# A four-layer graph network on one core: in the fourth layer, the products that sum ReLUs to scores go from the middle to the end of the first ten steps

## The chip, the core and the metric

The kernel runs on one core of a Trainium2 chip. The core has a matrix engine (TensorE, PE in the profile), a vector engine (VectorE, DVE), an engine for functions of one element (ScalarE, ACT), GpSimd (POOL) and queues that start transfers (SyncE, SP). Each engine works through its own list of instructions in order, and waits where an operand or a buffer is not ready. TensorE writes into PSUM, which has few banks; VectorE and ScalarE read the results from there ("evict" them) and so free the bank for the next product.

The metric is the device time of one execution in microseconds, as the median of several runs. Lower is better.

## The reference

Four layers are added to `x` (128 graphs of 64 nodes with 256 features) one after another. Each takes a layer norm and a ReLU of `x` first. The change is in the last one, graph attention over 512 edges with four heads:

```python
def _L3_gnn_ref(H, W_lin, W_val, a, W_out, A0, src, dst):
    Xq = (H @ W_lin.T).reshape(bt, n, h, dh)
    Xv = (H @ W_val.T).reshape(bt, n, h, dh)
    Qs = Xq[:, src]
    Kt = Xq[:, dst]
    e = jnp.einsum('behd,hd->beh', jax.nn.leaky_relu(Qs + Kt, LRELU_SLOPE), a)
    e = e + jnp.log(A0[src, dst] + EPS)[None, :, None]
    ...
    attn = ex / denom[src]
    Vt = Xv[:, dst].transpose(1, 0, 2, 3)
    Y = jax.ops.segment_sum(attn[..., None] * Vt, src, num_segments=n)
    Y = Y.transpose(1, 0, 2, 3).reshape(bt, n, d)
    return Y @ W_out.T
...
h = jnp.maximum(_layernorm(x, axis=-1), 0.0)
x = x + _L3_gnn_ref(h, L3_gnn_W_lin, L3_gnn_W_val, L3_gnn_a, L3_gnn_W_out, adj, L3_gnn_src, L3_gnn_dst)
```

`ex / denom[src]` is a softmax over the edges that leave one node. A leaky ReLU with slope 0.2 is 0.2 times its argument plus 0.8 times its ReLU, and the kernel uses it in that form.

## The kernel before

`x` lies in sixteen tiles X of 512 rows (128 partitions, four row blocks of 256). The fourth layer, `layer3` (L2439), runs 32 steps `g` of 256 rows, four graphs. Its parts, in the names that the trace shows:

- `score` (L2585): eight products of queries Q with an edge matrix (`ed_S2`, which adds the rows of source and target of each edge), each into a PSUM bank `ps` of its own, and eight ReLUs on ScalarE from `ps` to tiles `r`. There are seven `ps` banks and eight `r` tiles.
- `reduce` (L2606): eight products that multiply each `r` with the weights `a` (`ed_apad`) and add the result into the PSUM bank `acc`. Each has a stationary operand of 32 columns, so four stand side by side in the array. Eight steps share one `acc`; the first of the eight opens it. There is one such bank.
- `summed` (L2687), after every eighth step: one more product adds the linear part (`lin`) to `acc` and closes it. `softmax` (L2674) then reads `acc` with two scans, a maximum and a subtraction on VectorE (`sm_m`, `sm_e`, in `shifted`, L2691), takes Exp on ScalarE, and goes on with scans and reciprocals on VectorE.
- `edgewise` (L2703): two steps later `sm_e` is transposed and copied to `at`. `between` (L2715), `weighted` (L2743) and `output` (L2759) use it: VectorE spreads `at` over edges into tiles `aw`, TensorE gathers them (`aw` with `ed_ODT`), weights the values, and multiplies with the output matrix `w_o`. They lag ten steps behind (`LAG`, L2455; `v = g - LAG`), so in the first ten steps none of them runs.
- `back` (L2281): the layer before leaves its result in another layout (`big`). In each of steps 0 to 7 the next block is copied to `ls_t` (half on VectorE, half on ScalarE), transposed on TensorE (`ident` with `ls_t`) and added to X on VectorE. This is called the way back.
- `turned` (L2505), in even steps: the normed rows `h` are transposed (`ident` with `h`) to `hT`, one half evicted by VectorE and the other by ScalarE, and VectorE makes the sums `hS`.
- `queries` (L2535), in odd steps: queries and values of the next block from `hT` and `hS`, seven pairs of products by one level of Strassen-like sums, whose evictions go partly into each other (`XV`, `Q`). Its second half, `rest`, follows after `output` and `edgewise`, and ends with `linear` (L2569), which makes `lin`.
- `normed` (L2600), in odd steps: the layer norm of a later block (`n_st`, `n_mv`, `n_v`, `n_y` by Sqrt on ScalarE, `n_r`, `n_m`, then `h`).

In a step of the first ten the calls are `score`, `normed`, `reduce`, `summed` (step 7), `back` (steps 0 to 7), `turned` or `queries`, `edgewise` (step 9), `rest`, `softmax` (step 7).

The order on each engine comes from a scheduler that the tile framework runs over the whole program. It may take later instructions of another engine's list forward where operands allow; on TensorE the order of `layer3` is largely that of the calls. Buffers rotate in the order in which the program asks for them: an allocation of a `ps` bank waits for the readers of the one seven allocations earlier. The products of `reduce` take none of these seven.

Every operation is recorded through one helper, so nearly all lines of the profile say L799; one goes by the names of the tiles.

Of the kernel before, what the change touches and what calls it, by code (L numbers as in the profile page):

```python
# [842 lines left out]
class Plan:  # L843
# [56 lines left out]
    def rest(self):  # L900

        while any(self.queue.values()):
            for e in self.queue:
                self.fill(e, 1e9)
# [545 lines left out]
NG = 4  # L1450
# [15 lines left out]
class Kernel:  # L1466
# [972 lines left out]
    def layer3(self):  # L2439
        nc, o, io = self.nc, self.o, self.io  # L2440
        cx, (w,) = self.stage([("l3x", 1)], "tile")
        with cx:
            cy, pools = self.stage([("l3", 2), ("l3v", 2), ("l3s", 1), ("l3r", 6), ("l3ps", 7), ("l3cps", 1)], "tile")
            with cy:
                self.a02 = self.everywhere(w, "ed_a", io["L3_gnn_a"].rearrange("h d -> (h d)"))
                o.ts(self.a02[:], self.a02[:], 0.2, ALU.mult)
                self.drop, self.dropr = (w.tile([P, E], F32, name="ed_" + n) for n in ("drop", "dropr"))
                WQV = w.tile([P, 2, 2 * D], F32, name="w3_qv")
                for x, n in enumerate(("W_lin", "W_val")):
                    nc.sync.dma_start(WQV[:, :, x * D:(x + 1) * D],  # L2450
                                      io[f"L3_gnn_{n}_t"].rearrange("(k p) m -> p k m", p=P))
                WO = self.weights(w, "w3_o", io["L3_gnn_W_out_t"])


                st, LAG = {}, 10  # L2455
                self.turned(st, 0, *pools)
                WQV = self.sums3(w, WQV)
                self.queries(st, 0, WQV, *pools)()
                for g in range(8 * NG):
                    v = g - LAG  # L2460
                    ahead = (g + 1) // 2 if g % 2 and g + 1 < 8 * NG else None
                    self.score(st, g, *pools)
                    if g % 2 and g + 3 < 8 * NG:
                        self.normed(st, (g + 3) // 2, pools[0])
                    if v >= 1:
                        self.weighted(st, v - 1, *pools)
                    self.reduce(st, g, *pools)
                    if g == 4:
                        self.drops()
                    if v >= 0:  # L2470
                        self.between(st, v, *pools)
                    if g % 8 == 7 and g + 1 < 8 * NG:
                        self.summed(st, g // 8, *pools)
                    if g < 8:
                        self.back(8 + g, pools[4], "ps")
                    if ahead:
                        rest = self.queries(st, ahead, WQV, *pools)
                    elif g + 2 < 8 * NG:
                        self.turned(st, g // 2 + 1, *pools)
                    if g + 6 == 8 * NG:  # L2480

                        p = pools[4].tile([P, BT], F32, name="ps")
                        for c in range(4):
                            self.nc.tensor.transpose(p[:N, c * P:(c + 1) * P], self.OST[:, c, :], self.ident[:])
                        self.act_copy(self.cont[:N, :], p[:N, :])
                    if v >= 1 and g + 1 < 8 * NG:
                        self.output(st, v - 1, WO, *pools)
                    if g % 8 == 1 and 1 < g:
                        self.edgewise(st, g // 8 - 1, *pools)
                    if ahead:  # L2490
                        rest()
                    if g % 8 == 7 and g + 1 < 8 * NG:
                        self.softmax(st, g // 8, *pools)
                self.turn(st, WO, pools)
# [342 lines left out]
```

## Time and profile before

| | us |
|---|---|
| runs of the kernel before, median of 3 | 2264.54 |
| lowest and highest of them | 2262.23, 2266.95 |
| profiled execution | 2267.39 |
| its span | 2265.6 |
| fourth layer from the scores of step 0 to the end of the span | 1754.07 to 2265.6 |
| scores of step 10 begin | 1863.60 |

The profile lists, for each engine, how long it was busy, which groups of instructions cost most, who waited for whom, and the chain of work that ended last. A line of the timeline gives start, length, engine, source line, operation, output and inputs, tile shape and count, and in brackets the idle time before it with what ended it. Several products in a row are one line; their lengths overlap a little, so the distance from one line's start to the next one's is what a group takes. One product in float32 shows as two records.

The windows of the first ten steps, two steps to a row (columns: window, its length, busy time and instructions of PE, PEld, DVE, ACT and POOL, granted clock, share of the transfer engines, GB/s):

```profile
1754.07:1775.63 21.56, 21.56 (x117) 12.25 (x116) 13.17 (x33) 15.43 (x27) 0.00 (x0) 1.00 0.00 1
1775.63:1797.20 21.57, 21.57 (x117) 12.25 (x116) 14.55 (x36) 13.88 (x26) 0.00 (x0) 1.00 0.00 1
1797.20:1818.77 21.57, 21.57 (x117) 12.25 (x116) 14.13 (x34) 13.88 (x26) 0.00 (x0) 1.00 0.00 1
1818.77:1842.12 23.35, 23.01 (x119) 12.46 (x118) 16.29 (x36) 14.76 (x27) 0.00 (x0) 1.00 0.00 1
1842.12:1863.60 21.48, 20.18 (x105) 10.71 (x104) 18.46 (x42) 13.54 (x26) 0.00 (x0) 1.00 0.00 0
```

TensorE is busy throughout in the first three rows; the clock is full, and transfers play no part. The last two rows hold the first softmax.

### The profile page before, as it was taken

What the parts mean: (1) busy time and instruction counts of PE and PEld (TensorE: products, weight loads), DVE (VectorE), ACT (ScalarE), POOL (GpSimd) and SP (SyncE); (2) the same over time, 40 slices, a digit from 0 to 9 for tenths busy, and PEclk for the clock granted to TensorE, in tenths of its full rate; (3) what the DMA queues carried; (4) which work ended last, traced back from release to release, by engine and by line L of the source; (5) the groups of instructions that cost most, each with busy time, mean ns of one, the idle gap of its engine ahead of it and who ended that gap; (6) DMA issues with size and microseconds to landing.
All of it is one profiled execution on the core that took longest, in us unless ns stands there. A gap on an engine that the chain in (4) does not pass through costs nothing.

```text
span 2265.6 us, 33653 instructions
## 1 busy us (share of the span) xinstructions
PE 2222.2 (98%) x12617; PEld 1619.5 (71%) x12617; DVE 1611.1 (71%) x4068; ACT 1143.9 (50%) x2499; POOL 7.3 (0%) x33
## 2 busy tenths in 40 slices
PE   7999998999999999999999999999999999999999
PEld 4554444667777778888999999888887555555554
DVE  8877576888438786676766766666965688778667
ACT  5667864764436663444444444334533664444431
POOL 1000000000000000000000000000000000000000
PEclk9999999999999999999999999999999999999999
DMA  6000210121000000000100002000002000000001
GB/s 180 1 1 13 73 56 23 66 94 38 1 28 1 1 19 1 1 1 1 38 1 1 1 1 75 1 1 5 13 1 75 1 1 15 15 20 20 15 25 48
DMA packets 61070, 54.88 MB, mean 24 GB/s; under 512 B 15203, under 2 KB 58724, under 8 KB 60900
## 3 DMA queue, kind: packets, MB, share of 16 engines
q1 hardware_dynamic: 60900, 52.66, 7.5%
q8 instruction: 101, 1.65, 0.3%
q14 instruction: 69, 0.57, 0.1%
HBM read 35.86 MB, written 16.78 MB: 23 GB/s over the span
## 4 chain that ended last, share of the span: by engine, by line
PE 78%; DVE 4%; ACT 1%; issue 1%; ACTq 0%; DVEq 0%
PE ps L799 71%; PE pt L799 4%; PE acc L799 3%; DVE sm_m L799 1%; PE pe L799 1%; DVE aw L799 1%; DVE X L799 1%; DVE XV L799 0%; ACT ls_g L799 0%; ACT h L799 0%; DVE ls_g L799 0%; DVE lin_p L799 0%; DVE lin_s L799 0%; DVE hT L799 0%; DVE sm_e L799 0%
## 5 line engine op out<-in xcount | busy, mean ns | idle before, releaser
L799 ACT ACTIVATE ls_g<-ls_g,ls_b 128x512 f32<-128x512 f32 (+4 forms) x472 | 243.2, 565 | 154.7 <-DVE ls_g L799 152.9
L799 ACT ACTIVATE ls_g<-ps,ls_b 128x256 f32<-128x256 f32 (+3 forms) x268 | 115.3, 470 | 335.6 <-PE ps L799 332.5
L799 PE MATMUL ps<-z,w 128*128 128x512 f32 x512 | 257.2, 624 | 0.0
L799 PE MATMUL ps<-big,X 128*128 128x176 f32 (+3 forms) x848 | 212.7, 366 | 0.1
L799 DVE TENSOR_TENSOR ls_g<-ls_z,ps 128x512 f32<-128x512 f32 (+5 forms) x256 | 146.9, 579 | 91.6 <-PE ps L799 90.0
L799 PE MATMUL ps<-ls_tx,X 128*128 128x160 f32 (+2 forms) x960 | 206.8, 326 | 1.5 <-DVE ls_tx L799 0.9
L799 PE MATMUL ps<-X,X 128*128 128x160 f32 (+1 forms) x896 | 199.0, 306 | 0.0
L799 PE MATMUL ps<-X,ls_w 128*128 128x256 f32 x640 | 190.4, 379 | 0.0
L799 PEld LDWEIGHTS ps<-ls_tx,X 128*128 128x128 f32 x960 | 161.7, 190 | 16.4 <-DVE X L799 4.8
L799 DVE TENSOR_TENSOR aw<-at,ed_OST 128x1024 f32<-128x1024 f32 x128 | 150.3, 1219 | 28.7 <-PE ps L799 28.5
L799 PEld LDWEIGHTS ps<-big,X 128*128 128x128 f32 x848 | 146.0, 190 | 29.7 <-issue 19.4
L799 ACT ACTIVATE r<-ps 128x512 f32<-128x512 f32 x256 | 129.3, 625 | 63.0 <-PE ps L799 63.0
L799 DVE TENSOR_TENSOR X<-ls_g 128x1024 f32<-128x1024 f32 (+2 forms) x108 | 117.4, 1087 | 49.8 <-ACT ls_g L799 49.8
L799 PEld LDWEIGHTS ps<-X,X 128*128 128x128 f32 x896 | 148.5, 190 | 0.0
L799 PE MATMUL ps<-X,ls_s 128*128 128x256 f32 x480 | 142.3, 379 | 0.0
L799 PEld LDWEIGHTS ps<-z,w 128*128 128x128 f32 x512 | 87.6, 191 | 67.8 <-issue 60.6
L799 PE MATMUL ps<-ls_tx,ls_s 128*128 128x256 f32 x464 | 134.7, 379 | 0.0
L799 PEld LDWEIGHTS ps<-X,ls_w 128*128 128x128 f32 x640 | 121.4, 190 | 16.8 <-DVE X L799 0.3
L799 PE MATMUL ps<-ls_tx,ls_w 128*128 128x256 f32 x464 | 133.3, 380 | 0.1
L799 PE MATMUL ps<-big,ls_w 128*128 128x256 f32 x464 | 131.9, 379 | 0.8 <-ACT ls_z L799 0.8
L799 PE MATMUL ps<-ed_S,Q 64*128 64x512 f32 x512 | 121.4, 604 | 2.2 <-DVE hT L799 1.3
L799 PE MATMUL ps<-aw,ed_ODT 128*32 128x512 f32 x1024 | 121.7, 593 | 0.1
(552 smaller groups left out, 3946.4 us busy)
## 6 DMA issues: line engine op xcount, KB each, us to landing
X<-in_x_dram SPq DMA_DIRECT2D x32, 512.0 KB
xs<-X SPq DMA_DIRECT2D x16, 512.0 KB
X<-xs SPq DMA_DIRECT2D x16, 512.0 KB
out_dram<-X SPq DMA_DIRECT2D x31, 256.0 KB
X<-in_L_gnn_Wih_t_dram SPq DMA_DIRECT2D x4, 512.0 KB
ls_w<-in_L_gnn_Wih_t_dram SPq DMA_DIRECT2D x4, 512.0 KB
ls_w<-in_L_gnn_Whh_t_dram SPq DMA_DIRECT2D x4, 512.0 KB
w<-in_L_gnn_W_t_dram SPq DMA_DIRECT2D x2, 512.0 KB
```

The source lines that it names most:

```text
L799: i = method(*a, **kw)
```

## The change

In the steps in which nothing lags behind (`v < 0`, that is `g` from 0 to 9), `reduce` is called after `rest`, as the last work of the step on TensorE; in step 7 `summed` follows it there. From step 10 on the order is the old one. Nothing is computed differently.

```diff
                     if v >= 1:
                         self.weighted(st, v - 1, *pools)
-                    self.reduce(st, g, *pools)
+                    if v >= 0:
+                        self.reduce(st, g, *pools)
                     if g == 4:
                         self.drops()
                     if v >= 0:
                         self.between(st, v, *pools)
-                    if g % 8 == 7 and g + 1 < 8 * NG:
+                    if v >= 0 and g % 8 == 7 and g + 1 < 8 * NG:
                         self.summed(st, g // 8, *pools)
                     if g < 8:
                         self.back(8 + g, pools[4], "ps")
...
                         self.edgewise(st, g // 8 - 1, *pools)
                     if ahead:
                         rest()
+                    if v < 0:
+                        self.reduce(st, g, *pools)
+                        if g == 7:
+                            self.summed(st, 0, *pools)
                     if g % 8 == 7 and g + 1 < 8 * NG:
                         self.softmax(st, g // 8, *pools)
```

The scheduler's list moves other engines' work too. In the changed kernel's issue order ScalarE takes the first softmax's table load and Exp after the third ReLU of step 8 (before: ahead of all eight), and the first query eviction comes ahead of the normed rows `h`. VectorE runs the first softmax nearly without other work between its pieces, and copies `hT` ahead of the four reciprocals (before: behind them).

## The prediction

> **What bounds the kernel now.** I read the page first: TensorE is busy almost all the time, and the chain that ended last runs on it.
>
> ```profile
> PE 2222.2 (98%) x12617; PEld 1619.5 (71%) x12617; DVE 1611.1 (71%) x4068; ACT 1143.9 (50%) x2499; POOL 7.3 (0%) x33
> PE 78%; DVE 4%; ACT 1%; issue 1%; ACTq 0%; DVEq 0%
> ```
>
> A busy TensorE can still be one that crawls, so next I read the timeline of TensorE and ScalarE in the first ten steps of the fourth layer (1754.07 to 1863.60 us). Steps 0 and 1, then step 9 and a block of later steps:
>
> ```profile
> 1754.07 3.70 PE L799 MATMUL ps<-ed_S,Q 64*128 64x512 f32 x16
> 1757.70 2.74 PE L799 MATMUL acc<-r,ed_apad 128*32 128x512 f32 x16
> 1760.38 1.09 PE L799 MATMUL ps<-ident,ls_t 128*128 128x128 f32 x8
> 1761.31 1.04 PE L799 MATMUL ps<-ident,h 128*128 128x128 f32 x8
> 1762.27 3.70 PE L799 MATMUL ps<-ed_S,Q 64*128 64x512 f32 x16
> 1765.91 2.73 PE L799 MATMUL acc<-r,ed_apad 128*32 128x512 f32 x16
> 1768.56 1.09 PE L799 MATMUL ps<-ident,ls_t 128*128 128x128 f32 x8
> ...
> 1755.32 4.03 ACT L799 ACTIVATE r<-ps 128x512 f32<-128x512 f32 x8 [2.66 <-PE ps L799]
> 1763.51 4.03 ACT L799 ACTIVATE r<-ps 128x512 f32<-128x512 f32 x8 [0.39 <-PE ps L799]
> ...
> 1898.04 3.82 PE L799 MATMUL ps<-aw,ed_ODT 128*32 128x512 f32 x32
> 1901.79 1.09 PE L799 MATMUL ps<-ident,h 128*128 128x128 f32 x8
> ...
> 2219.12 1.99 PE L799 MATMUL ps<-w_o,y 128*128 128x256 f32 x8
> 2221.04 3.64 PE L799 MATMUL ps<-aw,ed_ODT 128*32 128x512 f32 x32
> 2224.61 0.69 PE L799 MATMUL ps<-an,XV 64*64 64x64 f32 x32
> ```
>
> Eight ReLUs take 4.03 us, 0.504 each, and start 1.24 us behind the scores. The last one of step 0 ends at 1755.32+4.03 = 1759.35, and the sum (acc) ends at 1757.70+2.74 = 1760.44, 1.09 later; in step 1 it is 1767.54 and 1768.64, 1.10 later. The sums follow ScalarE, though the trace calls TensorE busy. How short they are unhindered, the same tile shape with operands ready shows: 32 records of aw take 3.75 us from start to start (1898.04 to 1901.79), 3.57 at 2221.04; 16 are 1.79 to 1.88. The waits between engines name this too, but only in part, since a slow record counts as busy:
>
> ```profile
> PEld acc L799 <- ACT r L799: 9.6, 36, 0.4
> ```
>
> Two further places in steps 7 to 9 matter:
>
> ```profile
> 1840.92 0.68 DVE L799 TENSOR_TENSOR sm_e<-acc,sm_m 128x512 f32<-128x512 f32 x1
> 1853.61 1.13 PE L799 MATMUL ps<-ed_S,Q 64*128 64x512 f32 x4 [1.30 <-DVE hT L799]
> 1855.91 1.28 ACT L799 ACT_TABLE_LOAD   x1
> 1857.20 0.20 ACT L799 ACTIVATE n_y<-n_v 128x4 f32<-128x4 f32 x1
> ```
>
> **The change, part by part.** No instruction is added or taken out: ten groups of eight products, and one product that closes the first softmax, move to the end of their step. They issue no transfer, so SP's and POOL's queues stay. I take step lengths from start to start.
>
> *Steps 0 to 6.* A sum takes 2.67 us now (1757.70 to 1760.38, 1765.91 to 1768.56). Moved, it has 1.9 us (even steps: two groups of transposes) or 7.1 us (odd steps: way back and queries) of other products ahead of it. The ReLUs end 1.24+4.03 = 5.27 us into the step; in an even step the sum starts at 3.64+0.93+0.96 = 5.53, so all are ready. I take 1.87 us for it. Its bounds are 1.79 (above) and 2.27, the sum of step 9 (from 1854.66 to 1856.92), which is itself held by its last ReLU. Entering this tile shape from full-size products costs a bit: w_o takes 1.92 us ahead of aw (2219.12 to 2221.04) and 1.73 ahead of its own shape, so 0.19, where scores are entered for 0.09 (last products of the queries: 0.955 against 0.865). I charge 0.10 more per step. Gain: 2.67-1.87-0.10 = 0.70 per step, 7 steps, 4.9 us.
>
> The Trainium skill, TensorEngine Tiling (Array Packing), section Key Properties, says that a change of tiling mode drains the engine. That speaks against a free move: at the 0.10 of the rows it is in the sum already, at a full pass it is rival C below. The number of changes stays three per step; only their order is new, and no row has sums directly ahead of scores.
>
> *What the sums covered.* In odd steps they gave ScalarE and VectorE 2.67 us to clear the ReLUs before the queries' evictions. Now, in step 3: ReLUs end at 5.27, then the Sqrt, half a way back (about 1.05) and the first query eviction, done at about 6.9; VectorE's two additions of 0.6 end at 8.3. The product that needs the second starts at 3.64+0.93+0.87+1.73+1.72 = 8.89. Cover left: 0.5 us; nothing is charged. In step 1 a table load of 1.28 stands behind the ReLUs, and one more VectorE piece between the two additions: they end at 9.1, 0.27 late. Charged: 0.27. The values' last additions and Q come 1.9 us before the next scores instead of right before them.
>
> *Steps 7 to 9.* From the scores of step 7: 3.64+0.93+6.14+0.10+1.87, plus 0.96 for the closing product, 13.64. VectorE is by then at its query sums and free at 13.93; two scans (1.13 each), small copies (0.3), maximum and subtraction (0.6 each, plus hand-over) end at 17.95, and Exp at 18.58. In the changed issue order ScalarE has that table load and Exp between the third and the fourth ReLU of step 8. So the other five end at 18.58+5x0.504 = 21.15 with hand-over, and the sum of step 8 ends 1.09 later, 22.24, instead of 13.64+3.64+0.96+1.87 = 20.1: a new wait of 2.1 us. Behind it stand the scores of step 9, 22.2 to 25.84. VectorE meanwhile goes on from Exp: two scans and a product (3.0), the copy of hT, four reciprocals (3.37), three more pieces, so the second query product waits to 27.55 (0.85 more). From there 5.6 us of products (0.43 of them the transposes of the softmax) and the sum (1.97): scores of step 10 at 35.15. Now it is 1863.60-1826.99 = 36.61. This stretch gains 1.46: three short sums, the 1.30 at 1853.61 and some 0.9 in step 7 (its queries take 7.01, 1835.11 to 1842.12, against 6.14) pay for the new waits.
>
> The ScalarE page of the Trainium skill (ScalarE: Activation LUTs, What ACT_TABLE_LOAD costs) counts a drain of 1.38 us with each table switch. The row disagrees: the load at 1855.91 starts 0.01 after the last ReLU and Sqrt follows at 1857.20. By the page Exp would be 1 us later and the gain of the whole change 5.1.
>
> *After step 10* each engine stands to TensorE as before within 1 us: the fourth aw ends 6.5 us behind the scores (now 6.8). TensorE is at 99.5% and more to 2215, so the lead carries to the end.
>
> Sum: 4.9-0.27+1.46 = 6.1 us. The profiled execution took 2267.39 (span 2265.6 and 1.8 around it) and would be 2261.3. It lies 2.85 above the median of the runs shown, 2264.54, to which the forecast goes: **2258.4 us**.
>
> **Rivals.**
> - *The sum is no shorter (B).* If 2.27 us is what it takes even with all ReLUs there, 0.4 a step goes from seven steps and from step 9: 6.1-3.2 = 2.9, so 2261.6. For it: no row of before shows this sum with every ReLU long done. Against: both short ones end 1.09 behind a ReLU, and aw with the same shape runs at 1.8.
> - *Drains (C), the other side.* Sums between full-size products and half-height scores: each change of shape drains for a whole pass (0.59 us, a record of acc) instead of 0.1 to 0.19. At entry and exit 0.5 more each, 1.0 a step, 9 of 10 steps: 9 us against 6.1, slower by 2.9, 2267.4. It decides from 0.34 us a change. For it: the adjacent pair is new. Against: aw to transposes, also out of this shape, adds 0.18 at most (3.75 against 3.57).
> - *Softmax late (D).* VectorE needed 7.2 us from the first scan (1834.44) to the end of the subtraction (1841.60), with other work between; I count 4.0. At 7.2, Exp and the sum of step 8 come 3.2 later: 2.9 is left, 2261.6. Against: in the changed order almost nothing stands between.
> - *That it doesn't do what it says* is excluded by the issue order: the sums do stand behind transposes and queries.
>
> **How the numbers follow.** No change is what lies within 0.2%, 4.5 us, about what the three runs spread. Forecast 70%, of it 4% under 4.5 us of gain; B 8%; C 12%; D 10%, of it 2% above 4.5 us (a delay half as long). Faster 66+2 = 68%, same 4+8+8 = 20%, slower 12%. The forecast's own range is 2255 to 2260.5: sum at 1.79 or 2.1, and step 8 off by 1.5 us either way. B and D belong in the range, with a run's spread of 2 us: 2254.8 to 2264.0, leaving out C and a little at the low end.
>
> **What would show it.** Right: in steps 0 to 7 acc takes 1.8 to 2.0 us from start to start; a pair of steps takes 20.2 instead of 21.57; no waits of TensorE in odd steps save step 1; the sum of step 8 waits about 2 us for the ReLUs behind Exp; from step 10 on the trace is the old one, shifted. Wrong: acc at 2.2 or more (B), scores or transposes next to it longer by 0.3 or more (C), the subtraction later than 4.5 us behind the first scan (D), or query products waiting for additions in steps 3 and 5, which would mean that the cover of 0.5 us was not there.

## The result, and the profile after

| | before | after |
|---|---|---|
| median of the runs, us | 2264.55 (10 runs) | 2257.6 (10 runs) |
| lowest and highest | 2261.45, 2268.06 | 2255.41, 2260.57 |
| profiled execution | 2267.39 | 2258.33 |
| its span | 2265.6 | 2256.5 |
| scores of step 0 to scores of step 7 | 72.92 | 67.54 |
| scores of step 7 to scores of step 10 | 36.61 | 35.37 |
| scores of step 10 to the end of the span | 402.0 | 401.93 |

The changed kernel takes 0.997 of the time before, 95% interval 0.9962 to 0.9978: 0.3% faster, 5 to 8.6 us of 2264.5.

The two profiled executions lie further apart, 9.1 us in their spans. That isn't all the change: the fourth layer begins at 1754.07 in the one and at 1751.66 in the other, though nothing is changed ahead of it. Beginnings of this layer lay between 1748.85 and 1754.86 in all the profiled executions of this study. The change's whole lead of 2.41 there is already present 42 us into the execution (last section). So what the change does is read from the start of the scores of step 0 to that of step 10, where the order of TensorE's work differs: 109.53 us before, 102.91 after, 6.62 less. With the 2.41 of the beginning and 0.07 of the rest, that is the 9.1.

TensorE's timeline of the changed kernel, steps 0 to 2 (start, length, engine, line, operation, output and inputs, shape, count):

```profile
1751.66 3.70 PE L799 MATMUL ps<-ed_S,Q 64*128 64x512 f32 x16
1755.29 1.09 PE L799 MATMUL ps<-ident,ls_t 128*128 128x128 f32 x8
1756.22 1.04 PE L799 MATMUL ps<-ident,h 128*128 128x128 f32 x8
1757.19 1.92 PE L799 MATMUL acc<-r,ed_apad 128*32 128x512 f32 x16
1759.04 3.70 PE L799 MATMUL ps<-ed_S,Q 64*128 64x512 f32 x16
...
1766.20 1.89 PE L799 MATMUL ps<-w_qv,hT 128*128 128x256 f32 x8
1768.15 1.13 PE L799 MATMUL ps<-w_t,hT 128*128 128x256 f32 x4
1769.12 1.03 PE L799 MATMUL ps<-w_qv,hS 128*128 128x256 f32 x4
1770.08 1.92 PE L799 MATMUL acc<-r,ed_apad 128*32 128x512 f32 x16
1771.93 3.70 PE L799 MATMUL ps<-ed_S,Q 64*128 64x512 f32 x16
```

Each sum (acc) is as many products as before and takes 1.85 us from start to start (1757.19 to 1759.04, 1770.08 to 1771.93) instead of 2.67. Scores take 3.63 (1751.66 to 1755.29) as before, and the products right before the sum 0.97 and 0.96, as before. The view of weight loads, which names what a late operand held up, shows the same for the stretch from the scores of step 0 to those of step 10 (us in all, times, longest; before, then after):

```profile
PEld acc L799 <- ACT r L799: 8.8, 33, 0.4
```

```profile
PEld acc L799 <- ACT r L799: 2.2, 5, 0.8
PEld ps L799 <- ACT r L799: 8.7, 11, 1.1
```

The second line of after is no new loss: ten of the eleven waits, 0.76 us each, are of loads that stand behind scores, and TensorE multiplies without a gap meanwhile. The eleventh is at the wait in step 9 shown below.

Nearly all of what is left sits in one place, step 8. The changed kernel's timeline, TensorE and then ScalarE, steps 8 and 9:

```profile
1837.47 3.98 PE L799 MATMUL acc<-r,ed_apad 128*32 128x512 f32 x16
1841.38 3.70 PE L799 MATMUL ps<-ed_S,Q 64*128 64x512 f32 x16
...
1846.85 1.97 PE L799 MATMUL ps<-w_t,hS 128*128 128x256 f32 x8 [0.71 <-DVE hS L799]
...
1834.08 1.57 ACT L799 ACTIVATE r<-ps 128x512 f32<-128x512 f32 x3 [5.20 <-PE ps L799]
1835.67 1.28 ACT L799 ACT_TABLE_LOAD   x1
1837.29 0.63 ACT L799 ACTIVATE sm_e<-sm_e 128x512 f32<-128x512 f32 x1 [0.33 <-DVE sm_e L799]
1837.82 2.53 ACT L799 ACTIVATE r<-ps 128x512 f32<-128x512 f32 x5
```

Three ReLUs, the table load and Exp of the softmax, then the other five ReLUs, the last ending at 1837.82+2.53 = 1840.35. The sum ends 1.10 later, at 1837.47+3.98 = 1841.45. It took 3.91 us, 2.05 more than the 1.86 of other steps, and again TensorE counts as busy meanwhile. One step further a query product waits 0.71 for the sums hS, behind the softmax on VectorE.

### The profile page after: what moved, and what is told of

It is laid out like the page before. It is cut to its first block, busy times and chain, and to the rows that moved or that the text cites. A ratio compares the mean times of both kernels' runs of the same rounds, so it can differ in the third digit from the quotient of the medians.

```text
span 2256.5 us, 33659 instructions
## 1 busy us (share of the span) xinstructions
PE 2213.2 (98%) x12617; PEld 1615.1 (72%) x12617; DVE 1609.3 (71%) x4068; ACT 1142.8 (51%) x2499; POOL 7.2 (0%) x33
## 4 chain that ended last, share of the span: by engine, by line
PE 77%; DVE 4%; ACT 1%; issue 1%; ACTq 0%; DVEq 0%
PE ps L799 70%; PE pt L799 4%; PE acc L799 3%; DVE sm_m L799 1%; PE pe L799 1%; DVE aw L799 1%; DVE X L799 1%; DVE XV L799 0%; ACT ls_g L799 0%; ACT h L799 0%; DVE ls_g L799 0%; ACT r L799 0%; DVE hT L799 0%; DVE lin_s L799 0%; DVE lin_p L799 0%
```

## The experiments

The theory: a sum that stands right behind its scores is as long as ScalarE makes it; moved away from them it is 1.86 us, and what is left in its place is a wait in step 8, where Exp has slipped between the ReLUs. Rivals: the place matters for another reason (changes of tile shape, other work that moves along), or the sums save less and the steps of the softmax save more. The table gives starts of scores on TensorE's timeline, as the lengths of two stretches, and the ratio of the runs to those of the kernel before on the same chip.

| kernel | steps 0 to 6 | steps 7 to 9 | both | ratio, 95% interval |
|---|---|---|---|---|
| before | 72.92 | 36.61 | 109.53 | |
| the change | 67.54 | 35.37 | 102.91 | 0.9970, 0.9962 to 0.9978 |
| 1: only steps 0 to 6 | 67.55 | 36.61 | 104.16 | 0.9971, 0.9959 to 0.9984 |
| 2: behind the way back | 70.31 | 36.76 | 107.07 | 0.9996, 0.9987 to 1.0006 |
| 3: two ReLUs on VectorE | 70.31 | 39.23 | 109.54 | 0.9999, 0.9989 to 1.0009 |
| 4: step 7 in the old place | 67.54 | 35.57 | 103.11 | 0.9966, 0.9956 to 0.9976 |
| 5: before, a ninth ReLU | 75.99 | 36.55 | 112.54 | 1.0008, 0.9999 to 1.0018 |
| 6: the change, a ninth ReLU | 68.40 | 35.36 | 103.76 | 0.9977, 0.9967 to 0.9987 |
| 7: all steps | 67.55 | 35.37 | 102.92 | 0.9978, 0.9968 to 0.9988 |
| 8: Exp behind the ReLUs | 67.55 | 34.41 | 101.96 | 0.9960, 0.9947 to 0.9974 |
| 9: as 3, to step 6 | 70.31 | 36.61 | 106.92 | 0.9991, 0.9981 to 1.0001 |
| 10: as 8, transposes later | 67.54 | 34.45 | 101.99 | 0.9955, 0.9939 to 0.9972 |

**1. Only steps 0 to 6.** The diffs are against the changed kernel unless they say otherwise.

```diff
-                    if v < 0:
+                    if g < 7:
                         self.reduce(st, g, *pools)
-                        if g == 7:
-                            self.summed(st, 0, *pools)
```

(and the conditions of the old place to match).

> Only steps 0 to 6 have their sums at the end; steps 7 to 9 are as before. From the scores of step 0 to those of step 10 it was 109.53 us before and 102.91 with the whole change; to the scores of step 7 it was 72.92 and 67.54. Theory (each moved sum no longer runs behind its last ReLU): 67.5 to step 7, then 36.6 as before, 104.1 in all, 5.4 us faster than before. Rival (more than half of the gain comes from the other order of softmax, ReLUs and hT in steps 7 to 9): 3 us faster at most, 106.5 or more.

67.55 and 36.61 us: the two parts of the change add up, and each is worth what the changed kernel's stretches say: 5.4 and 1.24.

**2. Behind the way back.** The sums leave the scores, but go ahead of the transposes and the queries.

```diff
                         self.back(8 + g, pools[4], "ps")
+                    if v < 0:
+                        self.reduce(st, g, *pools)
+                        if g == 7:
+                            self.summed(st, 0, *pools)
...
                         rest()
-                    if v < 0:
-                        self.reduce(st, g, *pools)
-                        if g == 7:
-                            self.summed(st, 0, *pools)
```

> In the first ten steps the sums go behind the way back only, ahead of transposes, queries and values; the first softmax starts in mid-step 7 again. Theory: the sum starts at 3.64+0.93 = 4.57 us, the ReLUs end at 5.27, and the last four products of the sum start after 5.4, so 0.9 us of other work is cover enough: 1.86 us a sum in steps 0 to 7, no wait in step 1, 67.2 to step 7. Steps 8 and 9 have no way back, so their sums stay ReLU-bound (2.6 and 2.3). In all about 103, 6.5 faster than before. Rival (the whole of transposes and queries is needed as cover): sums of 2.2 or more and 2 to 3 us of the gain lost, 105.5.

107.07, worse than either theory. The timeline of run 2, TensorE in step 3, then ScalarE:

```profile
1786.37 1.09 PE L799 MATMUL ps<-ident,ls_t 128*128 128x128 f32 x8
1787.39 1.92 PE L799 MATMUL acc<-r,ed_apad 128*32 128x512 f32 x16
1789.25 1.13 PE L799 MATMUL ps<-w_qv,hT 128*128 128x256 f32 x4
...
1794.00 1.13 PE L799 MATMUL ps<-w_t,hT 128*128 128x256 f32 x4 [0.17 <-DVE XV L799]
...
1795.93 3.70 PE L799 MATMUL ps<-ed_S,Q 64*128 64x512 f32 x16
...
1789.74 2.07 ACT L799 ACTIVATE h<-X,n_m,n_r 128x256 f32<-128x256 f32 x4 [0.60 <-DVE n_m L799]
1791.72 0.57 ACT L799 ACTIVATE XV<-ps 128x512 f32<-128x512 f32 x1
```

The sum is short here too (1787.39 to 1789.25, 1.86): that half of the theory holds in a second place. But the queries take 6.68 us (1789.25 to 1795.93) where they took 6.14. In this kernel's order ScalarE makes four rows h before it evicts the first query product (XV at 1791.72), VectorE's additions come late, and the product of w_t and hT waits (it starts 2.06 us behind the group ahead of it, 1.73 in step 3 of the change). There is also one change of tile shape more in a step: the transposes of ls_t take 1.02 (1786.37 to 1787.39) ahead of the sum, 0.93 ahead of other full-size products, the first query product 0.96 behind the sum instead of 0.87, and even steps, which have no queries, take 7.53 instead of 7.38 (starts of scores at 1775.20 and 1782.73). What the expectation missed is that moving TensorE's work also moves the scheduler's order of the evictions; in the change it put XV ahead of h.

**3 and 9. Faster ReLUs instead of a later sum.** Against the kernel before: in each step the fourth and the eighth ReLU go to VectorE, in run 3 for ten steps, in run 9 for seven (`g < 7`).

```diff
-                    self.act(r[:], ps[x][:], AF.Relu)
+                    if g < 10 and k == 2 and x == 1:
+                        self.o.ts(r[:], ps[x][:], 0.0, ALU.max)
+                    else:
+                        self.act(r[:], ps[x][:], AF.Relu)
```

> The order is that of before; in the first ten steps two of the eight ReLUs (the fourth and the eighth) go to VectorE. Theory (the sum ends 1.09 behind the last ReLU): the last ReLU ends at about 4.5 us in odd steps and 4.7 in even ones, where VectorE still makes query sums, instead of 5.27; sums end at 5.6 to 5.8 instead of 6.36, 0.55 to 0.8 a step, 104 to 105 from step 0 to step 10. Rival (what helped is the place of the sums: other neighbours, fewer or cheaper changes of tile shape): sums of 2.6 as before, 109.5.

> The order of before; the fourth and the eighth ReLU on VectorE in steps 0 to 6 only, so that no ReLU stands behind the softmax on VectorE. Theory (the loss of the run with ten such steps came from VectorE's ReLUs behind its softmax): scores of step 0 to scores of step 7 in 70.3 us as there, from step 7 to step 10 36.6 as before, 106.9 in all, 2.6 less than before. Rival (splitting the ReLUs delays VectorE's work by itself, and the softmax with it): 38 to 39.2 from step 7 to step 10, 108.5 to 109.5 in all.

The timeline of run 3, TensorE in steps 0, 1 and 8, then VectorE in step 8:

```profile
1755.37 2.42 PE L799 MATMUL acc<-r,ed_apad 128*32 128x512 f32 x16
1757.72 1.09 PE L799 MATMUL ps<-ident,ls_t 128*128 128x128 f32 x8
...
1763.25 1.97 PE L799 MATMUL acc<-r,ed_apad 128*32 128x512 f32 x16
1765.15 1.09 PE L799 MATMUL ps<-ident,ls_t 128*128 128x128 f32 x8
...
1843.62 1.93 PE L799 MATMUL acc<-r,ed_apad 128*32 128x512 f32 x8 [2.45 <-DVE r L799]
...
1842.90 0.67 DVE L799 TENSOR_SCALAR r<-ps 128x512 f32<-128x512 f32 x1
1843.48 3.38 DVE L799 RECIPROCAL sm_m<-sm_m 128x128 f32<-128x128 f32 x4
1846.77 0.63 DVE L799 TENSOR_SCALAR r<-ps 128x512 f32<-128x512 f32 x1
```

In step 1 the sum takes 1.90 us without having moved at all, in step 0 2.35, where VectorE is at other work. So it is the ReLUs that set it, not its place. The gain in steps 0 to 6 is 2.61 us, 0.37 a step, less than the 0.55 to 0.8 expected: in even steps VectorE reaches its two ReLUs late, and step 2 even takes 8.31 us instead of 8.21. Run 3 gave the 2.6 us back in steps 7 to 9: a ReLU queued on VectorE comes after the softmax's scans, the next one after its four reciprocals, and the sum waits 2.45 us. Run 9 ends the split before the softmax: 70.31 and 36.61, 106.92 us as the theory had it; the rival, 38 or more in steps 7 to 9, falls.

**4. Step 7 in the old place.**

```diff
-                    if v < 0:
+                    if v < 0 and g != 7:
                         self.reduce(st, g, *pools)
-                        if g == 7:
-                            self.summed(st, 0, *pools)
```

(and the old place for step 7).

> As the change, but step 7 keeps its sum and the closing product in the old place, so the softmax starts early and Exp stands ahead of all ReLUs of step 8. Theory: 67.5 to step 7; the sum of step 8 is 1.9 instead of 3.9, but hT is copied behind the reciprocals again, and the scores of step 9 wait for it, so the lead is lost there; 36.2 for steps 7 to 9, 103.7 in all, 0.8 slower than the change. Rival (the wait behind Exp is a loss of its own that can be had back): 2 us faster than the change, 100.9.

35.57 us, 0.2 behind the change, less than the theory had counted. TensorE's timeline of run 4 in step 8 and at the start of step 9:

```profile
1838.71 1.92 PE L799 MATMUL acc<-r,ed_apad 128*32 128x512 f32 x16
1840.56 2.85 PE L799 MATMUL ps<-ed_S,Q 64*128 64x512 f32 x12
1844.76 1.13 PE L799 MATMUL ps<-ed_S,Q 64*128 64x512 f32 x4 [1.35 <-DVE hT L799]
```

The wait in the sum of step 8 is gone (1.85), and step 9 waits 1.35 for the copy of hT, which this order puts behind the softmax again, so that a bank comes free late. The runs don't tell this kernel from the change (0.9966 and 0.9970). So the sum of step 7 gains little by its move. In the change step 7 is 1.51 shorter than here (13.62, 15.13) and step 9 0.74 (13.19, 13.93), but step 8 is 2.05 longer (8.56, 6.51), because the softmax begins later.

**5 and 6. A ninth ReLU.** In steps 0 to 6 the fifth ReLU is made twice, in the kernel before and in the changed one.

```diff
                     self.act(r[:], ps[x][:], AF.Relu)
+                    if g < 7 and fc and k == 0 and x == 0:
+                        self.act(r[:], ps[x][:], AF.Relu)
```

> The order of before; in steps 0 to 6 the fifth of the eight ReLUs is made twice (the same result written again), 0.50 us more on ScalarE a step. Theory (sum ends 1.09 behind the last ReLU): every sum of steps 0 to 6 is 0.5 longer, 72.92 + 3.5 = 76.4 us to step 7 and 113.0 to step 10. Rival (TensorE itself takes this long for the sum): no longer than before, 109.5.

> The changed order with the same second ReLU in steps 0 to 6. Theory: the sums do not see it (even steps: the last ReLU ends at 5.8, the last half of the sum starts at 6.4). In odd steps ScalarE reaches the first query eviction 0.5 later, where the changed kernel had 0.34 to 0.40 us of cover (step 3) and none in step 1: 0.1 to 0.2 in steps 3 and 5, 0.5 in step 1, so 67.54 + 0.8 = 68.3 to step 7. Rival (odd steps pass a late ReLU on in full): 69.0 or more.

TensorE's timeline of run 5, the sum of step 0 and what follows it:

```profile
1752.49 3.23 PE L799 MATMUL acc<-r,ed_apad 128*32 128x512 f32 x16
1755.65 1.09 PE L799 MATMUL ps<-ident,ls_t 128*128 128x128 f32 x8
```

The same of run 6, with the wait of step 1:

```profile
1757.23 1.92 PE L799 MATMUL acc<-r,ed_apad 128*32 128x512 f32 x16
1759.08 3.70 PE L799 MATMUL ps<-ed_S,Q 64*128 64x512 f32 x16
...
1768.61 1.13 PE L799 MATMUL ps<-w_t,hT 128*128 128x256 f32 x4 [0.48 <-DVE XV L799]
```

The ninth ReLU costs ScalarE 0.48 us (nine take 4.51 in step 0 of run 5, eight 4.03). It lengthens each step of the old order by 0.44 on average ((75.99-72.92)/7), and the sums of the new order not at all (1757.23 to 1759.08 is 1.85). In the new order it costs 0.86 us in seven steps, half of it in step 1, where the queries' evictions were late already: 13.31 us (1759.08 to the scores of step 2 at 1772.39) against 12.89 in the change. This test separates the cause best: the same work added, 3.07 us in the one order and 0.86 in the other.

**7. All steps.** `reduce` and `summed` stand at the end of every step.

```diff
-                    if v < 0:
-                        self.reduce(st, g, *pools)
-                        if g == 7:
-                            self.summed(st, 0, *pools)
+                    self.reduce(st, g, *pools)
+                    if g % 8 == 7 and g + 1 < 8 * NG:
+                        self.summed(st, g // 8, *pools)
```

> The sums of all steps go to the end of their step, also those from step 10 on. Theory: from step 10 the sum already has weighted values ahead of it and the gathering of aw behind it in the same tile shape, which runs on while the last ReLU's product ends (1.74 us from start to start), so nothing is to be had: about 0.1 longer a step for the added changes of shape and new waits like that of step 8 at the second and third softmax, 2 to 6 us slower than the change, about 2261. Rival (every moved sum gains 0.8): 21 steps, 15 us faster than the change, about 2242.

The first ten steps are the change's (102.92). From the scores of step 10 to the end it takes 404.88 us, 2.95 more than the 401.93 of the change. TensorE's timeline of run 7 at the second softmax:

```profile
1950.43 0.69 PE L799 MATMUL ps<-an,XV 64*64 64x64 f32 x30 [1.81 <-ACT r L799]
...
1956.98 1.96 PE L799 MATMUL ps<-w_o,y 128*128 128x256 f32 x8 [1.27 <-DVE y L799]
```

From step 10 on other products stand between scores and sums already, so there is hardly a late ReLU to hide: ordinary steps are 0.04 to 0.08 us shorter than in the change, not 0.1 longer as expected. The loss is at the second and third softmax, which the later sums push back: steps 16 and 24 take 3.39 and 3.26 us more, of which the steps behind them give back 1.56 and 1.39.

**8. Exp behind the ReLUs.** The Exp of the first softmax, and what follows it there, are asked for in step 8 behind the transposes, and the scheduler is told to hold Exp behind ScalarE's eviction of hT.

```diff
                         self.turned(st, g // 2 + 1, *pools)
+                    if g == 8:
+                        self.softmax2(st, 0)
...
         e, m, m2 = self.shifted(st, q, pool, vp, sp, rp, psum, psc)
+        st["sm"] = e, m, m2
+        if q:
+            self.softmax2(st, q)
+
+    def softmax2(self, st, q):
+        nc, o = self.nc, self.o
+        e, m, m2 = st["sm"]
+        if not q:
+            nc.hold((None, None, nc.mark()[2]))
+            self.act(e[:], e[:], AF.Exp)
+            nc.hold()
...
-        self.act(e[:], e[:], AF.Exp)
+        if q:
+            self.act(e[:], e[:], AF.Exp)
```

> The changed order; in the first softmax Exp and what follows it are asked for in step 8, with Exp behind its eight ReLUs and the eviction of hT. Theory (2.05 us of wait in the sum of step 8 and 0.7 in the queries of step 9 come from Exp between the ReLUs and from hT behind the scans): the sum of step 8 takes 1.86, hT and hS are ready ahead of Exp, but the transposes of the softmax in step 9 now come 1 us too early; 33.7 instead of 35.37 us from the scores of step 7 to those of step 10, 101.2 in all, 1.7 faster than the change: 2255.9. Rival (the chain of the softmax on VectorE bounds steps 8 to 10 whatever the order): the wait only moves to the transposes of the softmax or to aw, 35.0 to 35.4.

34.41 us, between the two theories. The timeline of run 8 from step 8 on, TensorE, then VectorE:

```profile
1840.68 1.92 PE L799 MATMUL acc<-r,ed_apad 128*32 128x512 f32 x16
...
1851.28 0.63 PE L799 MATMUL ps<-ident,sm_e 128*128 128x128 f32 x4 [1.39 <-DVE n_r L799]
...
1850.44 0.69 DVE L799 TENSOR_TENSOR sm_e<-sm_e,sm_m 128x512 f32<-128x512 f32 x1
```

The sum of step 8 is 1.85 us (1840.68 to 1842.53) and the wait for hS is gone, as the theory said; TensorE now waits 1.39 for the transposes of sm_e, whose last factor ends on VectorE at 1850.44+0.69 = 1851.13. The profile names n_r there, the small piece that VectorE does next; what the transposes read is sm_e. Net gain over the change in this stretch: 0.96 us.

**10. Transposes later.** As 8, and the transposes of step 9 stand behind the second half of the queries (`edgewise` after `rest` where `g == 9`).

```diff
-                    if g % 8 == 1 and 1 < g:
+                    if g % 8 == 1 and 9 < g:
...
                         rest()
+                    if g == 9:
+                        self.edgewise(st, 0, *pools)
```

> The run with Exp behind the ReLUs, and besides the transposes of the first softmax in step 9 go behind the second half of the queries. Theory: TensorE no longer waits 1.39 us for the reciprocals ahead of the transposes, but the product of w_t and hT behind them waits for VectorE's addition to XV, which stands behind the softmax on VectorE in any case; so steps 7 to 9 take 34.4 to 34.9 us, as without this move. Rival (the transposes alone hold TensorE up): 33.0 to 33.3 us.

TensorE's timeline of run 10 in step 9:

```profile
1847.49 0.55 PE L799 MATMUL ps<-ident,sm_e 128*128 128x128 f32 x3 [0.20 <-DVE sm_e L799]
1849.27 1.13 PE L799 MATMUL ps<-w_t,hT 128*128 128x256 f32 x4 [1.24 <-DVE XV L799]
```

34.45 us, no gain: on TensorE three of the transposes came forward all the same, and now the query product waits 1.24 for VectorE's addition to XV, which stands behind the softmax's reciprocals and product. VectorE's queue holds these steps up, and this reorder of TensorE alone gave nothing more.

Runs 8 and 10 have the lowest ratios, 0.9960 and 0.9955, and their intervals lie wholly below 1. Against the change their intervals overlap; that they are ahead of it by 0.9 us is read from the stretch alone.

## Why the prediction was right, point by point

The mechanism holds, and the time of 2257.6 us lies beside the 2258.4 forecast. That they agree to 0.8 us is partly luck: the ten runs lie between 2255.41 and 2260.57, and the terms of the sum were off as follows.

- **Sums of steps 0 to 6.** The 2.67 us was ScalarE's time, shown by runs 3, 5, 6 and 9. The price taken for a sum unhindered, 1.87, measures 1.85.
- **The charge of 0.10 a step for the tile shape** was wrong. The products ahead of a sum take 0.96 to 0.97, as they did ahead of scores, and scores 3.63 behind a sum. The prediction read 0.19 at w_o as the price of entering the sum's shape. But w_o has a change on either side, since products of 64x64 stand ahead of it (before):

```profile
2218.49 0.69 PE L799 MATMUL ps<-an,XV 64*64 64x64 f32 x32
```

  So the 0.19 was for two changes. The last group of the queries, with one change behind it, takes 0.96 ahead of the sum of step 3 (1789.06 to 1790.02) and took 0.96 ahead of scores (1774.67 to 1775.63), against 0.86 for a group of this size ahead of its own shape (1788.20 to 1789.06). Per step the gain is 8.20-7.38 = 0.82 (step 0: 1754.07 to 1762.27, and 1751.66 to 1759.04), and seven times that is 5.74 where 4.9 was charged.
- **Step 1** was charged 0.27 and lost 0.34 (12.89 us long, step 3 12.55), at the product that the prediction named: 1766.20 to 1768.15 is 1.95 instead of 1.73 and the next ones follow it late. In step 3 VectorE's addition ended at 1787.80 and the product began at 1788.20, a cover of 0.40 where 0.5 was counted. Together 5.74-0.34 = 5.40; the stretch shows 5.38.
- **Steps 7 to 9** were to gain 1.46 and gained 1.24. Step 7 took 13.62 us (1819.20 to 1832.82; predicted 13.64), step 8 8.56 (predicted 8.60, with a wait in its sum of 2.05 for 2.1), step 9 13.19 (predicted 12.91). The miss is in step 9: the second query product began 27.65 us behind the scores of step 7 (predicted 27.55), and what follows it took 7.72 instead of 7.6.
- **Rival B**, a sum no shorter than 2.27, falls by the 1.85 or 1.86 of every step but step 8. **Rival C**, drains at the new neighbours, decided from 0.34 us a change; the new neighbours cost no more than the old ones here. One change more shows 0.10 in step 7, where the closing product now stands between sum and scores (1.06 us, 0.96 before), and 0.15 to 0.19 a step in run 2. The rule of the Trainium skill (TensorEngine Tiling (Array Packing), Key Properties) that such a change drains the engine gives no price; no run here shows more than these 0.19 us.
- **Rival D**, a late softmax, falls: first scan at 1833.11, the subtraction ends at 1837.25, 4.14 us where 4.0 was counted.
- **The table load.** The prediction set the row against the Trainium skill (ScalarE: Activation LUTs, What ACT_TABLE_LOAD costs), which counts a drain of 1.38 us. The changed kernel agrees with the row: the ReLUs end at 1834.08+1.57 = 1835.65, the load starts at 1835.67 and ends at 1836.95, and Exp then waits 0.33 for VectorE.
- **After step 10** the lead was to carry to the end, and it did: 401.93 us against 402.0.

Size for size, the misses partly cancelled: the sums gained 0.84 more than was said, step 1 and steps 7 to 9 brought 0.07 and 0.22 less, so 6.62 us where 6.1 was said. The runs' interval, 5 to 8.6 us, can't tell these apart; the stretch can.

## What to carry to other kernels

A matrix engine that the profile calls busy may be following another engine: set the end of its group beside the end of the last operand, and the group's length beside the same shape with operands long ready. Work put between producer and consumer hides the wait once, and only where nothing stood between; where products stood there already (run 7) the same move gained under 0.1 us a step and lost more at each softmax. And when work moves, read the order of evictions on the other engines anew, since runs 2, 3 and 10 lost or missed their gain there.

## What the runs showed of the hardware

- Between executions the granted clock of TensorE differs early on. Windows of 50 us of the kernel before, and then of run 5, which has the same order (columns as in the table of windows ahead of the prediction; the clock is the third from the right):

```profile
100.00:150.00 50.00, 48.84 (x224) 25.12 (x222) 39.27 (x194) 32.15 (x109) 0.00 (x0) 0.97 0.01 1
350.00:400.00 50.00, 40.74 (x183) 26.14 (x182) 31.68 (x164) 21.25 (x47) 0.14 (x1) 0.90 0.05 16
```

```profile
100.00:150.00 50.00, 48.85 (x224) 25.45 (x225) 40.48 (x201) 32.52 (x111) 0.00 (x0) 1.00 0.01 1
350.00:400.00 50.00, 39.04 (x195) 25.78 (x193) 33.28 (x167) 23.16 (x50) 0.14 (x1) 0.93 0.08 26
```

  TensorE's work ahead of the fourth layer is the same in both, in the same order. Run 5 begins that layer 5.22 us earlier (1748.85, 1754.07). An estimate from the clock is 0.03 of 50 us, twice, 3.0 us. The rest arises in the first 30 us, where the same group of z and w takes 6.28 us before (from 22.71) and 4.56 in run 5 (from 22.05), though the clock is given as 1.00 there for both.

  The same later product begins at 42.26 before, at 39.87 in run 5, 39.85 in the change and 42.63 in run 4. So the change has its whole lead of 2.41 there. Run 4 is 0.37 behind there and 2.69 ahead at the fourth layer (1751.38); it shows 1.00 and 0.93 in the two windows as run 5 does, the change 0.97 and 0.90. What makes the first products slower, and what sets the clock, stays open. For a change of 0.3% it means that spans of single profiles can't be compared, and stretches with the same start can.
- A change of the tile shape on TensorE cost little here: 0.10 us for one more in step 7 of the change, 0.15 to 0.19 a step in run 2, and nothing to be seen where only the order of the shapes was new.
